# The number of tiles in a register of every engine, and the last four of 39 tiles in a branch: a GRU and mixture-of-experts kernel

## The chip, the core and the metric

The kernel runs on one core of a Trainium2 chip. The metric is the device time of one execution in microseconds; the median of several executions is compared. TensorE (PE) multiplies, VectorE (DVE), ScalarE (ACT) and GpSimd (POOL) work elementwise, and SyncE (SP) and POOL issue most of the transfers. Each engine runs its own list of instructions in order and waits on semaphores that others raise.

## What is computed

The reference runs a GRU over 8 sequences of 256 steps with 512 features, and then a mixture-of-experts layer on all 2048 hidden states:

```python
probs = softmax(x @ w_gate)                      # 8 experts
topk_w, topk_ids = top_k(probs, 2)               # two experts for each token, weights normalized
gu  = einsum('th,ehf->etf', x, w_gate_up)        # 512 -> 2*256 for each expert
eo  = einsum('eti,eih->eth', silu(g) * u, w_down)
out = x_in + routed + shared                     # shared: one dense layer of width 1024
```

The kernel computes only the two chosen experts of each token: 4096 pairs of token and expert.

## The kernel before, in words

**The GRU stage** takes most of the time: 256 steps (`step`), and between the steps the projections of later inputs, the routing of the block of 16 steps before, and the shared layer of finished blocks.

**Routing.** For each block `give_places` gives every pair a place in its expert's list, and `enter` scatters (row number, weight) into `listed` in DRAM. Each list has room for all tokens. Vacant places were filled at the start with row numbers of runs of 16 neighbouring rows and weight 0 (lines 267 to 274).

**Laying tiles.** At the end `lay_tiles` cuts the eight lists into tiles of 128 pairs. With c pairs for an expert there are ceil(c/128) tiles, and their sum depends on the data; the largest possible sum is `NT` = 39. Part 0 counts (`cnt`), turns counts into tiles (`nte`), sums them up over the experts (`cum`, whose last column is the number of all tiles), finds for each of 128 partitions, taken as tile numbers, the expert (`ex`) and the place in the list (`at`), and gathers the lists (`nT`). Part 1 spreads the expert of each tile to all partitions with a matmul of ones and writes it as integers (`steer`). Part 2 transposes the gathered lists into `row` and `share`. A tile number past the last tile of the data gets expert 7 and a vacant list.

**The stage of tiles.** All 39 tiles are run, whether or not they hold tokens. `fetch_rows(i)` gathers 128 hidden states from DRAM by `row` (POOL, `xr`). `tile_unit(i)` makes four groups of work: `before_` transposes `xr` on PE (line 766), has ACT copy it to `xrT` (768) and fetches tile i + 2; then four up products `gu_t` (659), whose weights are chosen by a register of PE loaded from `steer` (774); `turn` transposes the gated activation (670, copy 672); the two down products `yp` (785), the weighting on DVE (788) and a scatter from POOL that adds the 128 rows to `out` in DRAM (791). Each scatter waits until the one before it has landed, since both add to the same tensor.

`run_tile` sets the order by hand: in one call it issues the first group of tile i, half of the up products of tile i-1, the turn of tile i-2, the other half, and the down products of tile i-2. Two last calls with nothing new run the pipeline empty. Lists are built by Python: the program is one straight sequence, and only which expert's weights are read is decided on the chip. After the last instruction SP waits for every semaphore, each engine drains, and a barrier of all engines ends the program (line 989).

Of the kernel before, what the change touches and what calls it, by code (L numbers as in the profile page):

```python
# [9 lines left out]
F32 = mybir.dt.float32  # L10
BF16 = mybir.dt.bfloat16
I32 = mybir.dt.int32
AF = mybir.ActivationFunctionType
ALU = mybir.AluOpType
# [3 lines left out]
P = 128  # L18
# [7 lines left out]
def kernel(  # L26
# [51 lines left out]
    nc = tc.nc  # L78
    B, T, D = x.shape
    G3 = w_ih.shape[1]  # L80
    E = w_gate.shape[1]
# [7 lines left out]
    NTOK = B * T  # L89
    NT = (2 * NTOK - E) // P + E  # L90
# [12 lines left out]
    ps_mm = ctx.enter_context(tc.tile_pool(name="ps_mm", bufs=3, space=PSUM))  # L103
# [84 lines left out]
    ident = const.tile([P, P], F32, name="ident")  # L188
# [101 lines left out]
    def for_transposes(shape, name):  # L290

        spare.rotate(-1)
        n = shape[0] * (shape[1] if len(shape) > 1 else 1)
        bank = spare[0][:, 0:n]
        return bank if len(shape) == 1 else bank.rearrange("p (a b) -> p a b", b=shape[1])
# [283 lines left out]
    laid = {}  # L579

    def small(shape, tag, dtype=F32):
        return two.tile([P, *shape], dtype, tag=tag, name=tag, bufs=1)

    def lay_tiles(part_no):

        if part_no == 0:
            ps = ps_mm.tile([P, E], F32, tag="mm", name="cntp")
            nc.tensor.matmul(ps, ones, count, start=True, stop=True)
            cnt = small([E], "cnt")
            nc.vector.tensor_copy(cnt, ps)  # L590
            more = small([E, NM], "parts")
            nc.vector.tensor_tensor(
                more,
                cnt.unsqueeze(2).broadcast_to([P, E, NM]),
                full.unsqueeze(1).broadcast_to([P, E, NM]),
                ALU.is_gt,
            )
            nt = small([E], "nte")
            nc.vector.tensor_reduce(nt, more, AX.X, ALU.add)

            ee = small([E, E], "ee")
            nc.vector.tensor_tensor(ee, upto, nt.unsqueeze(1).broadcast_to([P, E, E]), ALU.mult)
            cum = small([E], "cum")
            nc.vector.tensor_reduce(cum, ee, AX.X, ALU.add)

            past = small([E], "past")
            nc.vector.tensor_scalar(past, cum, part, None, ALU.is_le)
            ex = small([1], "ex")
            nc.vector.tensor_reduce(ex, past, AX.X, ALU.add)
            spread = small([NT], "spread", BF16)  # L610
            nc.vector.tensor_scalar(spread, ident[:, 0:NT], ex, None, ALU.mult)
            nc.vector.tensor_tensor(past, past, nt, ALU.mult)
            no = small([1], "no")
            nc.vector.tensor_reduce(no, past, AX.X, ALU.add)

            nc.vector.tensor_tensor(no, part, no, ALU.subtract)
            nc.vector.scalar_tensor_tensor(no, ex, float(NM), no, ALU.mult, ALU.add)
            at = small([1], "at", I32)
            nc.vector.tensor_scalar(at, no, float(E * NM), None, ALU.min)
            got = small([P, 2], "nT")  # L620
            nc.gpsimd.indirect_dma_start(
                out=got.rearrange("i p v -> i (p v)"),
                out_offset=None,
                in_=listed.rearrange("r p v -> r (p v)"),
                in_offset=bass.IndirectOffsetOnAxis(ap=at, axis=0),
            )
            laid.update(spread=spread, got=got)
        elif part_no == 1:
            ps = ps_mm.tile([P, NT], F32, tag="mm", name="exp")
            nc.tensor.matmul(ps, ones, laid["spread"], start=True, stop=True)  # L630
            steer = small([NT], "steer", I32)
            nc.vector.tensor_scalar(steer, ps, float(E - 1), None, ALU.min)
            laid["steer"] = steer
        else:
            ps = for_transposes([2, P], "listp")
            for v in range(2):
                nc.tensor.transpose(ps[:, v, :], laid["got"][:, :, v], ident)
            row = small([NT], "row", I32)
            nc.vector.tensor_copy(row, ps[:, 0, 0:NT])
            share = small([NT], "share")  # L640
            nc.vector.tensor_copy(share, ps[:, 1, 0:NT])
            laid.update(row=row, share=share)
# [106 lines left out]
    def fetch_rows(i):  # L749
        if i < NT:  # L750
            xr_of[i] = xpool.tile([P, D], F32, tag="x", name=f"xr_{i}")
            nc.gpsimd.indirect_dma_start(
                out=xr_of[i],
                out_offset=None,
                in_=rows.rearrange("b t d -> (b t) d"),
                in_offset=bass.IndirectOffsetOnAxis(ap=laid["row"][:, i : i + 1], axis=0),
            )

    def tile_unit(i):
        box = {}  # L760

        def before_():
            ps = for_transposes([NQ, P], f"xrTp_{i}")
            xr = xr_of.pop(i)
            for q in range(NQ):
                nc.tensor.transpose(ps[:, q, :], xr[:, q * P : (q + 1) * P], ident)  # L766
            xrT = two.tile([P, NQ, P], F32, tag="xrT", name=f"xrT_{i}")
            nc.scalar.copy(xrT, ps)  # L768
            box["xrT"] = xrT
            fetch_rows(i + 2)  # L770

        def weights(w):
            if "e" not in box:
                box["e"] = nc.values_load(
                    laid["steer"][0:1, i : i + 1],
                    engines=(mybir.EngineType.PE,),
                    min_val=0,
                    max_val=E - 1,
                )
            return we[:, bass.ds(box["e"], 1), w, :].rearrange("p o n -> p (o n)")  # L780

        def done(f, lhs, rhs):
            if f == 0:
                box["y"] = ps_mm.tile([P, D], F32, tag="mm", name=f"yp_{i}")
            nc.tensor.matmul(box["y"], lhs, rhs, start=(f == 0), stop=(f == NF - 1))  # L785
            if f == NF - 1:
                y = two.tile([P, D], F32, tag="y", name=f"y_{i}")
                nc.vector.tensor_scalar(  # L788
                    y, box["y"], laid["share"][:, i : i + 1], None, ALU.mult
                )  # L790
                nc.gpsimd.indirect_dma_start(  # L791
                    out=out.rearrange("b t d -> (b t) d"),
                    out_offset=bass.IndirectOffsetOnAxis(
                        ap=laid["row"][:, i : i + 1], axis=0
                    ),
                    in_=y,
                    in_offset=None,
                    compute_op=ALU.add,
                )

        return unit(
            f"t{i}",
            box,
            lambda q: box["xrT"][:, q, :],
            lambda q: weights(q),
            lambda f: weights(NQ + f),
            done,
            before_,
        )


    queue = deque()
    under_way = {"up": None, "turn": None}
# [10 lines left out]
    def run_tile(stages):  # L824


        last, oldest = under_way["up"], under_way["turn"]
        ups = last[1] if last else []
        for work in [
            *(stages[0] if stages else []),  # L830
            *ups[: NQ // 2],
            *(oldest[2] if oldest else []),
            *ups[NQ // 2 :],
            *(oldest[3] if oldest else []),
        ]:
            work()
        under_way.update(up=stages, turn=last)
# [94 lines left out]
    for e in (E - 4, E - 3):  # L932
# [3 lines left out]
        (0, choose), (MM, sum_logits), (2 * MM, order_experts), (2 * MM, weigh), (5 * MM, give_places),  # L936
        (5 * MM, lambda k: enter(k, 0)), (5 * MM, lambda k: enter(k, 1)), (6 * MM, send_rows),
        (7 * MM, lambda k: lay_tiles(0)), (8 * MM, lambda k: load_again(k - 1)),
        (8 * MM, load_again), (14 * MM, lambda k: lay_tiles(1)),
        (22 * MM, lambda k: lay_tiles(2)),  # L940
        (22 * MM, lambda k: fetch_rows(0)), (22 * MM, lambda k: fetch_rows(1)),
    ]
# [12 lines left out]
        if loads:  # L955
            loads.popleft()()
    assert not loads
    for i in range(NT):
        run_tile(tile_unit(i))
    for _ in range(2):  # L960
        run_tile(None)
    assert not any(under_way.values())


# [28 lines left out]
```

## Time and profile before

| what | value |
|---|---|
| median of 3 runs | 1509.24 us (1508.29 to 1509.33) |
| profiled execution | 1514.91 us, its span 1513.1 us |
| PE busy | 1443.1 us, 95% of the span |
| first tile's first transpose on PE | 1271.6 us after the span's start |
| last tile's `yp` ends on PE | about 1499.7 us |
| last scatter to `out` starts on POOL | 1503.5 us |
| granted PE clock in the stage of tiles | 1.00 |

The profiled execution took 5.67 us more than the median, and 1.8 us of its time lie outside its span. Times named by line come from that one execution. The stage of tiles and what follows it fill the last 241.5 us, 16% of the span.

### The profile page before, as it was taken

To read this page: it belongs to the slowest core of one execution; us is meant where nothing else is said; L and a number is where in the kernel's file an instruction comes from. 1 tells how busy PE (TensorE), PEld (TensorE's weight loads), DVE (VectorE), ACT (ScalarE), POOL (GpSimd) and SP (SyncE) were. 2 spreads that over 40 slices of the span, in tenths; PEclk is the share of its full clock that TensorE was granted. 3 is DMA by queue.
4 is the path that set the end of the run, shared out by engine and by line. 5 is a ranking of instruction groups with operands and counts; after the bars stand their busy time and mean duration, and the time that the engine had idled before them with its cause. 6 is when DMAs were issued, how large, how long until landed. Compare 5 with 4: busy or idle time off the path is not lost.

```text
span 1513.1 us, 75290 instructions
## 1 busy us (share of the span) xinstructions
PE 1443.1 (95%) x33154; PEld 1058.3 (70%) x33154; DVE 751.6 (50%) x2782; ACT 423.4 (28%) x1786; POOL 258.6 (17%) x505
## 2 busy tenths in 40 slices
PE   4699999999999999999999999999999999999996
PEld 1487777787778787777877777877787754444442
DVE  2356555655565656465655565556565541222221
ACT  0222222333332333333333333333333311222221
POOL 1122311111100001010101010101011221444442
PEclk8799999999999999999999999999999999999998
DMA  9244522122211011111101020111011332545453
GB/s 187 83 108 120 94 57 70 49 63 71 62 51 39 19 45 35 28 49 28 50 15 38 28 56 14 35 28 42 15 48 43 97 98 77 97 85 96 85 97 49
DMA packets 70122, 92.78 MB, mean 61 GB/s; under 512 B 13538, under 2 KB 46370, under 8 KB 69796
## 3 DMA queue, kind: packets, MB, share of 16 engines
q0 software_dynamic: 16352, 39.67, 12.9%
q1 hardware_dynamic: 53056, 48.14, 12.1%
q8 instruction: 261, 4.28, 1.2%
q14 instruction: 65, 0.53, 0.1%
q10 hardware_dynamic: 388, 0.16, 0.1%
HBM read 56.55 MB, written 31.37 MB: 58 GB/s over the span
## 4 chain that ended last, share of the span: by engine, by line
PE 90%; DMA 3%; DVE 3%; issue 2%; ACT 1%; SPq 0%; ACTq 0%; POOLq 0%; DVEq 0%; POOL 0%
PE ps_r L419 16%; PE ps_n L419 15%; PE gu_s L705 15%; PE ps_z L419 14%; PE gu_t L659 9%; PE gip L310 9%; PE po L310 7%; PE yp L785 4%; DMA we<-in_L_cond_W_hh_dram 1%; DVE zT L430 1%; DMA we<-in_L_cond_W_ih_dram 1%; DVE hn L454 0%; ACT z L449 0%; DVE hT L455 0%; PE ps_z L766 0%
## 5 line engine op out<-in xcount | busy, mean ns | idle before, releaser
L419 PEld LDWEIGHTS ps_r<-we,hT 128*8 128x8 f32 x8192 | 226.1, 89 | 119.3 <-ACT ps_z L403 72.7
L419 PE MATMUL ps_r<-we,hT 128*8 128x128 f32 x8192 | 280.8, 273 | 18.4 <-DVE hT L455 11.3
L419 PE MATMUL ps_n<-we,hT 128*8 128x128 f32 x8192 | 288.6, 273 | 1.0 <-issue 0.4
L419 PE MATMUL ps_z<-we,hT 128*8 128x128 f32 x8192 | 283.7, 273 | 2.4 <-issue 2.4
L705 PE MATMUL gu_s<-hc,wsu 128*32 128x256 f32 x4096 | 250.6, 379 | 1.2 <-issue 1.1
L458 POOL COPY hc<-hT 128x32 f32<-128x32 f32 x256 | 62.7, 245 | 1054.9 <-DVE hT L455 1052.3
L419 PEld LDWEIGHTS ps_n<-we,hT 128*8 128x8 f32 x8192 | 233.6, 90 | 8.3 <-issue 7.5
L419 PEld LDWEIGHTS ps_z<-we,hT 128*8 128x8 f32 x8192 | 234.7, 90 | 3.5 <-issue 3.3
L310 PE MATMUL gip<-we,xT 128*32 128x512 f32 (+1 forms) x1976 | 197.2, 508 | 29.5 <-DVE xT L299 22.0
L438 ACT ACTIVATE r<-rT 128x32 f32<-128x32 f32 x256 | 58.5, 229 | 521.5 <-DVE rT L430 521.5
L705 PEld LDWEIGHTS gu_s<-hc,wsu 128*32 128x32 f32 x4096 | 150.9, 110 | 76.0 <-issue 14.6
L430 DVE STREAM_TRANSPOSE rT<-ps_r 128x128 f32<-128x128 f32 x256 | 80.5, 314 | 190.5 <-PE ps_r L419 190.0
L659 PE MATMUL gu_t<-we,xrT 128*128 x312 | 146.7, 593 | 0.2 <-ACT xrT L768 0.2
L430 DVE STREAM_TRANSPOSE nT<-ps_n 128x128 f32<-128x128 f32 x256 | 80.9, 316 | 121.9 <-PE ps_n L419 121.8
L310 PE MATMUL po<-wsd,act_s 128*32 128x256 f32 (+1 forms) x1408 | 137.9, 476 | 0.0
L310 PEld LDWEIGHTS gip<-we,xT 128*32 128x32 f32 x1976 | 73.7, 111 | 82.0 <-issue 63.9
L403 ACT COPY ps_n<-seed_hn 128x128 f32<-128x128 f32 x256 | 68.8, 269 | 83.4 <-DVE nT L430 80.5
L650 DVE TENSOR_TENSOR act_t<-gu_t,act_t 128x256 f32<-128x256 f32 x39 | 16.6, 425 | 146.5 <-ACT act_t L649 146.5
L430 DVE STREAM_TRANSPOSE zT<-ps_z 128x128 f32<-128x128 f32 x256 | 81.1, 317 | 11.7 <-PE ps_z L419 3.9
L791 POOL DMA_INDIRECT out_dram<-y,row x39 | 61.8, 1585 | 124.5 <-DVE y L788 114.2
L446 ACT ACTIVATE nn<-nt 128x32 f32<-128x32 f32 x256 | 58.8, 230 | 81.0 <-DVE nt L444 79.6
L659 PEld LDWEIGHTS gu_t<-we,xrT 128*128 128x128 f32 x312 | 53.3, 190 | 38.7 <-issue 38.0
(160 smaller groups left out, 1204.6 us busy)
## 6 DMA issues: line engine op xcount, KB each, us to landing
gid_rz<-gi SPq DMA_DIRECT2D x16, 512.0 KB
seeds<-gid_rz SPq DMA_DIRECT2D x256, 32.0 KB
we<-in_L_ffn_w_gate_up_dram POOLq DMA_DIRECT2D x32, 256.0 KB, 3.7
gid_n<-gi SPq DMA_DIRECT2D x16, 256.0 KB
seeds_n<-gid_n SPq DMA_DIRECT2D x256, 16.0 KB
wsu<-_L_ffn_w_sh_gate_up_dram POOLq DMA_DIRECT2D x32, 128.0 KB, 3.6
rows<-hr SPq DMA_DIRECT2D x128, 32.0 KB
we<-in_L_ffn_w_down_dram POOLq DMA_DIRECT2D x16, 256.0 KB, 4.6
```

Source lines behind the costliest of these rows:

```text
L310: nc.tensor.matmul(ps[32 * c : 32 * c + 32], lhs(c), rhs, start=start, stop=stop, skip_group_check=True,)
L403: nc.scalar.copy(banks[g][:, 0:P], src[g])
L419: nc.tensor.matmul(bank[32 * j : 32 * j + B, 0:P], hT[:, q, 0:B], whh_v[:, q, a, j, :], start=False, stop=(q == NQ - 1), skip_group_check= ...
L430: nc.vector.transpose(gT.rearrange("p a b -> p (a b)"), banks[g][:, 0:P])
L438: nc.scalar.activation(r, gr, AF.Sigmoid)
L446: nc.scalar.activation(nn, nt, AF.Tanh)
L458: nc.gpsimd.tensor_copy(hc_of_block(k).rearrange("p g q (c t) -> p q g c t", t=TS)[:, :, :, :, t], new.rearrange("p q (g c) -> p q g c", c=2),
L650: nc.vector.tensor_tensor(act, ps[:, 0:IM], act, ALU.mult)
L659: nc.tensor.matmul(box["ps"], lhs(q), w_up(q), start=(q == 0), stop=(q == NQ - 1))
L705: nc.tensor.matmul(box["ps"][32 * g : 32 * g + 32, two_i, :], wsu[c][:, q, two_i, fs], hc_of[m][:, :, q, :], start=(two_i == 0 and q == 0) ...
L785: nc.tensor.matmul(box["y"], lhs, rhs, start=(f == 0), stop=(f == NF - 1))
L791: nc.gpsimd.indirect_dma_start(out=out.rearrange("b t d -> (b t) d"), out_offset=bass.IndirectOffsetOnAxis(ap=laid["row"][:, i : i + 1], a ...
```

## The change

The tile count, `cum[:, E-1]`, gets a place beside the experts: `spread` has one more column (the count in partition 0), the matmul of ones copies it to all partitions, and it becomes column 39 of `steer`. After everything else has been issued, and ahead of the tiles, every engine loads that integer into a register (`values_load` without a list of engines). The first 35 tiles (2048*2/128 + 3) are run as before and the pipeline is run empty. Then each engine compares its register with 35: if it is greater, tiles 35 to 38 are fetched and run, and otherwise the engine jumps past them. Tiles 33 and 34 no longer fetch tiles 35 and 36; the branch does.

```diff
-            spread = small([NT], "spread", BF16)
-            nc.vector.tensor_scalar(spread, ident[:, 0:NT], ex, None, ALU.mult)
+            spread = small([NT + 1], "spread", BF16)
+            nc.vector.tensor_scalar(spread[:, 0:NT], ident[:, 0:NT], ex, None, ALU.mult)
+            nc.vector.tensor_tensor(spread[:, NT:], ident[:, 0:1], cum[:, E - 1 : E], ALU.mult)
...
-            ps = ps_mm.tile([P, NT], F32, tag="mm", name="exp")
+            ps = ps_mm.tile([P, NT + 1], F32, tag="mm", name="exp")
             nc.tensor.matmul(ps, ones, laid["spread"], start=True, stop=True)
-            steer = small([NT], "steer", I32)
-            nc.vector.tensor_scalar(steer, ps, float(E - 1), None, ALU.min)
+            steer = small([NT + 1], "steer", I32)
+            nc.vector.tensor_scalar(steer[:, 0:NT], ps[:, 0:NT], float(E - 1), None, ALU.min)
+            nc.vector.tensor_copy(steer[:, NT:], ps[:, NT:])
...
-            fetch_rows(i + 2)
+            if i + 2 not in (always, always + 1):
+                fetch_rows(i + 2)
...
-    for i in range(NT):
-        run_tile(tile_unit(i))
-    for _ in range(2):
-        run_tile(None)
-    assert not any(under_way.values())
+    tiles = nc.values_load(laid["steer"][0:1, NT : NT + 1], min_val=1, max_val=NT)
+
+    def run_tiles(first, last):
+        for i in range(first, last):
+            run_tile(tile_unit(i))
+        for _ in range(2):
+            run_tile(None)
+        assert not any(under_way.values())
+
+    always = NTOK * 2 // P + 3
+    run_tiles(0, always)
+    with tc.If(tiles > always):
+        fetch_rows(always)
+        fetch_rows(always + 1)
+        run_tiles(always, NT)
```

The way around the branch is not empty in the built program. There every engine raises its own semaphores by what the skipped instructions would have added, and POOL does it for its transfers: it first waits until all of them have landed, then adds 16 to each of its eight transfer semaphores with one instruction. The waits at the end of the program count on these sums.

## The prediction

> **What bounds the kernel now.** I read the page first for which engine is busy at the end, then the stage of tiles by groups of instructions, then the chain of waits over its last tiles, and last the records of the closing line. The groups of instructions from 1265 us on (line, engine, operation, shapes, count | busy us, mean ns | idle time before and what ended it):
>
> ```profile
> L659 PE MATMUL gu_t<-we,xrT 128*128 x312 | 146.7, 593 | 0.2 <-ACT xrT L768 0.2
> L785 PE MATMUL yp<-we,actT_t 128*128 x156 | 73.4, 593 | 0.5 <-ACT actT_t L672 0.5
> L791 POOL DMA_INDIRECT out_dram<-y,row x39 | 61.8, 1585 | 124.5 <-DVE y L788 114.2 <-DMA out_dram<-y,row 6.7 <-issue 3.7
> L752 POOL DMA_INDIRECT xr<-rows,row x36 | 35.5, 987 | 23.1 <-PE ps_z L766 12.4 <-issue 10.7
> ```
>
> The reader sees PE with 0.7 us of waits in the whole stage, while POOL waits 114 us for DVE's `y`. So in this stage PE alone sets the pace, and it is the pace of 39 tiles, because `gu_t` and `yp` are counted for 39. The chain that ended last, in order of time (start us, us, who), shows one tile's length and what follows the last tile:
>
> ```profile
> 1478.26 1.72 PE yp L785 x4
> 1479.98 0.44 PE ps_z L766 x4
> 1480.41 1.72 PE gu_t L659 x4
> 1482.13 0.22 PE ps_r L670 x2
> 1482.35 1.72 PE gu_t L659 x4
> 1484.07 1.72 PE yp L785 x4
> ...
> 1495.25 1.73 PE yp L785 x4
> 1496.98 0.02 issue
> 1497.01 0.76 DVE y L788
> 1497.77 0.34 issue
> 1498.11 4.67 DMA out_dram<-y,row
> ```
>
> From `yp` to `yp` is 1484.07 - 1478.26 = 5.81 us. The chain ends in the last two scatters, one behind the other, and then in the closing line. Records of that line (line, queue, operation, count: ns min/median/max, first and last start us):
>
> ```profile
> L989 SPq EVENT_SEMAPHORE  x12: 17/28/28, 1508.0 to 1513.1; - x12
> L989 POOLq DRAIN  x3: 46/103/9010, 1503.3 to 1512.9; - x3
> L989 SPq DRAIN  x3: 7/7/7, 1508.6 to 1512.6; - x3
> ```
>
> SP's first wait ends at 1508.0, when the last scatter has landed (it started at 1503.5). Yet the program ends at 1513.1: POOL's long drain ends at 1503.31 + 9.01 = 1512.3, some 4.3 us after the landing, and the barrier waits for it.
>
> [...] scatter records last 1.55 to 1.64 us, landing takes 4.4 to 5.0.
>
> **How many tiles hold tokens.** The time turns on this and no profile shows it, so I take it from the inputs: the reference's own GRU and router give the eight experts 498, 438, 284, 598, 362, 852, 453 and 611 pairs. That is 4+4+3+5+3+7+4+5 = 35 tiles of 128. Thirty-five is not more than 35, so the branch is jumped over. For a 36th tile the fullest last tile (498 = 3*128 + 114) would need 15 pairs more; rounding in the products doesn't move that many.
>
> **The change part by part.**
>
> *Four tiles less.* Tiles 35 to 38 take 4 x 5.81 = 23.24 us out of PE's stretch, wholly on the path. With them go four gathers (4 x 0.99) and four scatters (4 x 1.59) on POOL, their transfers, and DVE's and ACT's part; these lay beside PE and gain nothing more. The last two tiles run the pipeline empty as tiles 37 and 38 did. **-23.24.**
>
> *The last two scatters carry tokens.* Before, the last two scatters belonged to vacant tiles, whose rows lie in runs of 16; they landed in 4.67 (chain) and about 4.4 us, the least of 39, against a median of 4.9. If tiles 33 and 34 take the median, the two links grow by 0.2 and 0.5. **+0.7** (0 to 0.9).
>
> *Two small DVE operations and a 40th column.* The product for `spread` is like its 128x1 neighbours, 0.16 us, ahead of `at` (ready 1238.9). The list gather that needs `at` starts only at 1241.6, since the last `enter` must land first: 2.7 us of cover. The copy into `steer` (0.15 us) comes at 1245.6, and DVE then idles 4.4 us. **0**; uncovered 0.3.
>
> *Five register loads.* PE already loads one register for each tile: 39 loads of 0.30 to 0.84 us, 0.40 in the median, which PE's sequencer makes ahead of its queue. The new one waits for `steer` (done at 1245.6) and stands ahead of tile 0's transposes, behind the last shared products; queued behind it are those transposes. The old load for tile 0 was made at 1269.4, 2.2 us before the transposes began at 1271.6, so 0.5 us more fits in; at worst +0.6. POOL's load stands ahead of the gather of tile 2, issued at 1259.2 and needed at 1276.0: 12 us of slack after 4.9 of flight is none lost. ACT's stands ahead of `xrT` of tile 0 (idle 5.35 us before it), DVE's ahead of tile 0's gating (idle 4.7 us), SP's and its range check behind its last transfer. **0.**
>
> *Moved fetches.* Gathers 35 and 36 leave tiles 33 and 34; jumped over, they are not issued. **0.**
>
> *The branch and the way around it.* PE, ACT and DVE reach it when their last work is queued, at the latest 0.8 us after `yp`[...]. SP sits there long before. POOL reaches it as its last scatter starts: 4.4 us of cover. What is exposed comes after the landing: POOL's wait for that landing, one more wait, the addition to eight semaphores, a branch. I estimate two waits at 0.06 (SP's ten waits took 0.54 us), the addition at 0.03[...]: **+0.2**. Behind it are SP's twelve waits (0.7 us), which now begin after POOL's addition; before, SP was done 0.6 us after the landing and waited 3.7 us for POOL's drain, so that drain still covers them.
>
> *The drain.* Before, it was queued while the last scatter was not yet issued; now it stands behind the landing. I take its end to stay 4.3 us behind the end of POOL's work: **0**. If it was only riding out the scatter, it becomes as short as the other two (0.1 us); SP's waits then end last, 1.0 us after the landing: -3.4. If it takes its 9.01 us anew from its new start: +4.7.
>
> **Sum:** -23.24 + 0.7 + 0.2 = -22.3. Against the profiled execution that is 1514.9 - 22.3 = 1492.6; that execution stood 5.7 us above the median, so I take the difference off the median: 1509.24 - 22.3 = **1486.9 us**.
>
> **The rivals.**
>
> *The drain vanishes behind POOL's new wait*: 1486.9 - 3.4 = 1483.5. For it: the drain has no work of its own that the page names. Against: 4.3 us after the landing something still ran. Chance 0.12.
>
> *The way around costs*: the drain anew[...]: up to 1486.9 + 4.7 = 1491.6. Chance 0.17.
>
> *The branch is taken* (the count on the chip is 36 or more, or the column holds something else), which ends slower. PE then runs empty at 1499.7 - 23.2 = 1476.5. POOL starts scatter 34 after 3.8 us, is busy 1.6, and only then can gather tile 35, 0.3 later; it lands after 5.4 (its median): 11.1 us without work on PE. Four tiles then take 4 x 5.81 + 1.5 (39 tiles took 1271.6 to 1499.7, 228.1 = 39 x 5.81 + 1.5), so `yp` ends at 1512.3, 12.6 us later than before: 1509.24 + 12.6 = 1521.8. It decides from the 36th tile on. The counts above speak against it. Chance 0.03.
>
> **How the numbers follow.** The forecast has 0.66; some 0.02 are for what none of these names. About 0.2%, 3 us, is what a measurement of this kernel can tell from no change; every case but the taken branch is beyond that on the fast side. The range goes from the vanished drain to the costly way round: 1483.4 to 1491.8. Faster 0.96, same 0.01, slower 0.03.
>
> **What would show it.** `gu_t` and `yp` counted for 35 tiles (x280 and x140), still 5.81 us from `yp` to `yp`, and the last `yp` ending near 1476.5 in the span. Five register loads besides 35 on PE, none with a wait of PE, ACT or DVE behind it. The last two scatters landing in about 4.9 us. After the last landing 5.3 us to the end of the span, POOL's long drain in it: 9 us or 1 us there decides between the first two rivals. Wrong at the root: x312 again, and a hole of 11 us in PE ahead of tile 35.

## The result, and the profile after

The changed kernel took **1489.09 us** in the median of four runs (1485.87 to 1490.79), the kernel before 1509.28 us beside it. The ratio is 0.9861 with a 95% interval of 0.9843 to 0.9879, that is 20.2 us less (18 to 24). The forecast was 1486.9 us, with a range of 1483.4 to 1491.8: faster, as forecast, by some 2 us less than forecast.

The two profiled executions (1485.87 and 1514.91 us) differ by 29 us, more than the medians do. Most of the surplus lies ahead of the tiles: the first transpose of tile 0 starts at 1263.1 us in the changed kernel and at 1271.6 us in the kernel before. A second profile of the kernel before has it at 1275.7, and two kernels below whose code is the old one up to that point have it at 1264.8 and 1275.1. I take the difference for chance between executions, since 7.7 of its 8.5 us are there already at the last GRU step, up to which the two programs have the same text, and since the kernel before took 1504.27 to 1510.12 us in eleven executions on one chip. It is not shown that the change has no part in it: where both kinds were profiled in one set, the changed front was the earlier one (1262.7 in e2 against 1264.8 in e1; 1271.5 in e7 against 1275.1 and 1275.7 in e6 and e8). The medians of three sets, 20.2, 21.7 and 20.3 us less than before, against the 20.9 that the stages add up to below, leave little room for a part of several microseconds. So I compare from that transpose on.

The groups of instructions of the changed kernel from 1257 us on, with the columns of the groups shown before:

```profile
L661 PE MATMUL gu_t<-we,xrT 128*128 x280 | 131.7, 593 | 0.2 <-ACT xrT L770 0.2
L788 PE MATMUL yp<-we,actT_t 128*128 x140 | 65.9, 593 | 0.5 <-ACTq L974 0.5
L794 POOL DMA_INDIRECT out_dram<-y,row x35 | 55.5, 1585 | 113.2 <-DVE y L791 95.9 <-DMA out_dram<-y,row 13.7 <-issue 3.7
L754 POOL DMA_INDIRECT xr<-rows,row x32 | 31.5, 985 | 21.0 <-PE ps_z L768 11.6 <-issue 9.4
```

The counts are those of 35 tiles (8 and 4 for each), one matmul takes 593 ns as before, and PE still waits only 0.7 us. The 0.5 us at `yp` are as long as before and named otherwise: the trace now puts them down to ACT's way around, whose semaphore record (1465.9) follows directly on ACT's last copy.

The chain of waits of the changed kernel over its last tiles (start us, us, who):

```profile
1452.34 1.72 PE yp L788 x4
...
1458.15 1.72 PE yp L788 x4
...
1463.52 1.73 PE yp L788 x4
1465.25 0.02 issue
1465.27 0.76 DVE y L791
1466.04 0.59 issue
1466.62 4.79 DMA out_dram<-y,row
```

A tile takes 1458.15 - 1452.34 = 5.81 us, unchanged, and the chain leaves PE for the last two scatters as it did before. New is what POOL does at the branch's line. Records of that line on POOL's queue (operation, count: ns min/median/max, first and last start us):

```profile
L974 POOLq EVENT_SEMAPHORE  x4: 17/43/43, 1472.1 to 1477.1; - x4
L974 POOLq COMPARE_BRANCH  x1: 53/53/53, 1471.9 to 1471.9; - x1
L974 POOLq INC_SWDGE_SEM  x1: 1319/1319/1319, 1477.2 to 1477.2; - x1
```

I read `INC_SWDGE_SEM` as the addition to the eight transfer semaphores. It starts 0.2 us after the last landing (1477.02) and takes 1.32 us. Then the closing line of the changed kernel:

```profile
L1004 SPq EVENT_SEMAPHORE  x14: 17/28/28, 1478.5 to 1484.0; - x14
L1004 POOLq DRAIN  x3: 46/103/4684, 1478.6 to 1483.8; - x3
```

SP's waits begin only when the addition is done (1478.5; before, at the landing), and POOL's long drain takes 4.68 us from there to 1483.25. From the last landing to the end there are 0.20 + 1.32 + 0.03 + 4.68 + 0.83 (the rest of the barrier) = 7.06 us, where the kernel before had 5.15.

The same four stretches, worked out from the records of each profiled execution (us; the landing is the last update of the scatter's semaphore):

| kernel | first transpose to last `yp` | `yp` to last scatter | its landing | landing to end |
|---|---|---|---|---|
| before | 228.09 | 3.85 | 4.44 | 5.15 |
| before, again (e8) | 228.09 | 3.84 | 4.79 | 5.15 |
| changed | 204.85 | 4.21 | 4.86 | 7.06 |
| changed, again (e2) | 204.85 | 3.75 | 4.79 | 7.06 |
| changed, third (e10) | 204.85 | 4.28 | 4.85 | 7.06 |
| 35 tiles written out (e1) | 204.85 | 3.85 | 4.88 | 4.83 |
| 35 tiles and an empty branch (e3) | 204.85 | 3.82 | 4.79 | 4.85 |
| branch in front (e4) | 206.29 | 3.85 | 4.82 | 4.85 |
| branch in front, gathers ahead (e5) | 204.87 | 3.91 | 4.84 | 4.85 |
| the same, again (e9) | 204.87 | 3.98 | 4.88 | 4.85 |
| 35 tiles, fills on POOL last (e6) | 204.85 | 4.11 | 4.79 | 13.66 |
| changed, fills ahead of the branch (e11) | 204.85 | 4.37 | 4.85 | 14.98 |
| branch taken (e7) | 243.71 | 3.95 | 4.63 | 5.18 |

The stretch of the tiles and the last column repeat to within 0.03 us between profiles of one kernel; the two in the middle scatter by half a microsecond.

### The profile page after: what moved, and what is told of

It reads as the page before. It is cut to its first block, busy times and chain, and to the rows that moved or that the text cites. A ratio compares the mean times of both kernels' runs of the same rounds, so it can differ in the third digit from the quotient of the medians.

```text
span 1484.1 us, 75080 instructions
## 1 busy us (share of the span) xinstructions
PE 1411.5 (95%) x33082; PEld 1029.6 (69%) x33082; DVE 744.3 (50%) x2772; ACT 418.2 (28%) x1774; POOL 248.0 (17%) x497
## 3 DMA queue, kind: packets, MB, share of 16 engines
q1 hardware_dynamic: 53056, 48.14, 12.6%
q8 instruction: 261, 4.28, 1.2%
## 4 chain that ended last, share of the span: by engine, by line
PE 90%; DMA 3%; DVE 3%; issue 2%; ACT 1%; SPq 0%; POOL 0%; DVEq 0%; ACTq 0%; POOLq 0%
PE ps_r L419 16%; PE gu_s L707 15%; PE ps_n L419 15%; PE ps_z L419 15%; PE gip L310 9%; PE gu_t L661 8%; PE po L310 7%; PE yp L788 4%; DMA we<-in_L_cond_W_hh_dram 1%; DMA we<-in_L_cond_W_ih_dram 1%; DVE zT L430 1%; DVE hn L454 0%; ACT z L449 0%; DVE hT L455 0%; PE ps_z L768 0%
## 5 line engine op out<-in xcount | busy, mean ns | idle before, releaser
L419 PEld LDWEIGHTS ps_r<-we,hT 128*8 128x8 f32 x8192 | 222.4, 89 | 120.8 <-ACT ps_z L403 72.0
L419 PE MATMUL ps_z<-we,hT 128*8 128x128 f32 x8192 | 279.3, 273 | 3.2 <-issue 3.2
L419 PE MATMUL ps_n<-we,hT 128*8 128x128 f32 x8192 | 277.9, 273 | 0.0
L419 PEld LDWEIGHTS ps_z<-we,hT 128*8 128x8 f32 x8192 | 229.8, 90 | 4.7 <-issue 4.3
L419 PEld LDWEIGHTS ps_n<-we,hT 128*8 128x8 f32 x8192 | 229.8, 90 | 0.2
L707 PEld LDWEIGHTS gu_s<-hc,wsu 128*32 128x32 f32 x4096 | 140.3, 110 | 84.8 <-issue 16.1
L310 PE MATMUL po<-wsd,act_s 128*32 128x256 f32 (+1 forms) x1408 | 134.2, 476 | 0.0
L661 PE MATMUL gu_t<-we,xrT 128*128 x280 | 131.7, 593 | 0.2 <-ACT xrT L770 0.2
L794 POOL DMA_INDIRECT out_dram<-y,row x35 | 55.5, 1585 | 113.2 <-DVE y L791 95.9
L403 ACT COPY ps_r<-seeds 128x128 f32<-128x128 f32 x256 | 67.0, 262 | 18.8 <-DMA seeds<-gid_rz 18.6
```

The lines of the kernel that those rows point to most:

```text
L310: nc.tensor.matmul(ps[32 * c : 32 * c + 32], lhs(c), rhs, start=start, stop=stop, skip_group_check=True,)
L403: nc.scalar.copy(banks[g][:, 0:P], src[g])
L419: nc.tensor.matmul(bank[32 * j : 32 * j + B, 0:P], hT[:, q, 0:B], whh_v[:, q, a, j, :], start=False, stop=(q == NQ - 1), skip_group_check= ...
L661: nc.tensor.matmul(box["ps"], lhs(q), w_up(q), start=(q == 0), stop=(q == NQ - 1))
L707: nc.tensor.matmul(box["ps"][32 * g : 32 * g + 32, two_i, :], wsu[c][:, q, two_i, fs], hc_of[m][:, :, q, :], start=(two_i == 0 and q == 0) ...
L794: nc.gpsimd.indirect_dma_start(out=out.rearrange("b t d -> (b t) d"), out_offset=bass.IndirectOffsetOnAxis(ap=laid["row"][:, i : i + 1], a ...
```

## Experiments: what the way around the branch costs

My theory after the result: the four tiles gave their 23.24 us, and the addition with the drain behind it took some 2 us back. The rivals: the loads and branches themselves cost something on the way, or the drain alone has grown.

**e1: 35 tiles written out, without loads and branch.** The kernel before with

```diff
-            fetch_rows(i + 2)
+            if i + 2 < 35:
+                fetch_rows(i + 2)
-    for i in range(NT):
+    for i in range(35):
```

It serves only data with at most 35 tiles, such as these.

> The kernel before with 35 tiles written into the program: no count, no register, no branch; tiles 35 to 38, which hold no tokens, are left out. It is the gain alone. If what the changed kernel gives back lies in the way around the branch (from the landing of the last scatter to the end of the span: 7.1 us in the changed kernel, 5.2 before), this one has 5.2 us there, and the PE stretch and the two last scatters of the changed kernel: about 1.9 us less than the changed kernel, 21.4 less than before. If the give-back came from elsewhere (the loads, the longer lists), the stretch after the landing is 7 us here too, or PE's stretch of tiles is shorter than the changed kernel's.

**e2: the changed kernel again**, on the same chip.

> The changed kernel once more, on the same chip as its comparisons. Expected: 20.5 us less than before by the stages (23.2 of PE less 0.8 of scatters less 1.9 after the landing), about 1488.8; if its profiled execution's 29 us less were the rule, 1480.

Measured: e1 1485.18 us, ratio to before 0.9855 (0.9838 to 0.9873); e2 1485.53 us, 0.9864 (0.9844 to 0.9883); before 1507.26. The medians, 0.35 us apart, can't tell the two apart, since the two intervals are over 5 us wide each. The profiles can: the stretch of the tiles is 204.85 us in both, and the landing is followed by 4.83 us in e1 (5.2 were expected) and 7.06 in e2. Ahead of the tiles, from the last GRU step's activation to tile 0's first transpose, they take 49.21 and 49.28 us. The closing line of e1:

```profile
L990 SPq EVENT_SEMAPHORE  x12: 17/28/28, 1478.4 to 1483.2; - x12
L990 POOLq DRAIN  x3: 46/103/9125, 1473.3 to 1482.9; - x3
```

Here the drain again stands ahead of the landing: queued at 1473.29, it ends at 1482.41, 4.02 us after the landing. So what the changed kernel has besides 35 tiles costs 7.06 - 4.83 = 2.2 us after the last landing, and no more than 0.1 us from the last GRU step to the tiles. Of the 2.2 us some 1.55 are the wait and the addition, and 0.66 come from the drain, which takes 4.68 us behind them instead of ending 4.02 us behind the landing.

**e3: the branch with next to nothing in it.** Loads, compares and jumps stay; the tiles in the branch are gone, and with them the transfers that the way around must make up for:

```diff
     with tc.If(tiles > always):
-        fetch_rows(always)
-        fetch_rows(always + 1)
-        run_tiles(always, NT)
+        nc.vector.memset(laid["share"], 0.0)
```

> The changed kernel with another branch body: one small memset on DVE in place of the four tiles (jumped over all the same, since 35 tiles hold tokens). The five loads, the five compares and the jump stay; POOL has no transfers to make up for. If the addition to the transfer semaphores and the drain behind it are what costs, the stretch from the last landing to the end is 5.2 us again, 1.9 less than in the changed kernel. If the compare and the jump[...] cost it, it stays near 7.

Measured in one run: 1480.98 us, with the first transpose as early as 1260.9, so the total says little. After the landing there are 4.85 us, as in e1, and the profile has no addition behind the tiles. Five loads, five compares and the jumps cost nothing that shows; the 2.2 us belong to what must be made up for when tiles are skipped.

**e6: work on POOL behind the last scatter.** Is the drain tied to the last scatter, or does it cost by itself? e1 with

```diff
+                if i == 34:
+                    for _ in range(14):
+                        nc.gpsimd.memset(y, 0.0)
```

after the scatter. The fills must wait until the scatter has read `y`, so they begin at the landing (in e11 below, which has the same fills, the first starts at 1477.77, 0.05 us after it).

> 35 tiles written in, and after the last scatter 14 memsets of its source tile on POOL, which must wait for the scatter's landing: POOL works some 5 to 8 us longer past the landing. It asks what POOL's long drain waits for. If it rides out something that the last scatter started (in four profiles it ended 8.8 to 8.9 us after that scatter began), the drain is short here, under 0.3 us, because that time has passed. If a drain costs over 4 us by itself once POOL has issued scatters, as the 4.7 us behind the addition in the changed kernel suggest, it ends over 4 us after the last memset.

Its closing line:

```profile
L993 POOLq DRAIN  x3: 46/103/5249, 1496.5 to 1502.3; - x3
```

The kernel took 1504.43 us in one run. The last fill ends at 1497.04, over 8 us after the landing (1488.90), and the drain at 1501.75. So the last drain ends 4.7 us behind POOL's last work, fills here and the addition in the changed kernel, also where the last transfer landed long before; it is not the rest of a transfer. It is no fixed price of every drain: POOL's drain at the start of the program takes 0.18 us, before and in the changed kernel. What the 4.7 us consist of stays open.

**e11: the same fills between the last scatter and the branch of the changed kernel.** The additions in e4 and e5 below took 0.73 and 0.79 us, so 1.32 could have contained a rest of the landing.

> The changed kernel with 14 fills of y (0.52 us each) on POOL between the last scatter and the branch, so that the addition comes some 8 us after the last landing. If the addition's 1.32 us is its own work, it stays at 1.3 us. If the half of it is a rest of the last transfer (the additions in front of the tiles took 0.73 and 0.79 us), it falls to 0.7 or 0.8 us. In both, the drain behind it takes 4.7 us, as it did behind the addition and behind the fills of the kernel of 35 tiles; should the drain follow the landing instead, it is under 1 us here.

One run took 1494.50 us. The addition, on POOL's queue at the branch's line:

```profile
L977 POOLq INC_SWDGE_SEM  x1: 1319/1319/1319, 1485.8 to 1485.8; - x1
```

and the drain on its closing line:

```profile
L1007 POOLq DRAIN  x3: 46/103/4684, 1487.2 to 1492.4; - x3
```

8.1 us after the landing both have the length they have in the changed kernel, 1319 and 4684 ns. So the addition's 1.32 us contain no rest of the landing. Why it is shorter ahead of the tiles is open.

## Experiments: the branch in another place, and the branch taken

**e4: the branch ahead of tile 0**, with the gathers of tiles 0 and 1 behind it, so that addition and landing would be over long before the end:

```diff
-        (22 * MM, lambda k: fetch_rows(0)), (22 * MM, lambda k: fetch_rows(1)),
...
-    run_tiles(0, always)
     with tc.If(tiles > always):
...
         run_tiles(always, NT)
+    fetch_rows(0)
+    fetch_rows(1)
+    run_tiles(0, always)
```

> The branch with tiles 35 to 38 stands ahead of tile 0 in place of behind tile 34; gathers 0 and 1 follow it. If the way around costs only because nothing runs beside it, it now lies under the last shared products on POOL (gather 0 had 10 us of slack), the stretch after the last landing is 5.2 us, and the kernel is 1 to 2 us faster than the changed one; PE pays for waiting until its own queue is empty, up to 1 us ahead of tile 0. If POOL's way round is longer than the slack, PE stands idle ahead of tile 0 by more than 2 us and nothing is won.

Measured: 1491.59 us (six runs), ratio 0.9904 (0.9885 to 0.9922), 6.1 us above e2 on the same chip. Who waited longest from 1255 to 1275 us in e4 (us in total, times, longest):

```profile
POOL xr L754 <- PEq L972: 26.1, 1, 26.1
...
PE ps_n L768 <- DMA xr<-rows,row: 6.7, 1, 6.7
```

The end is short again (4.85 us), but the gather of tile 0 waits for a semaphore that PE raises on its own way around the branch. PE's queue comes there only when the shared products are done, at 1262.9, so the gather is issued at 1263.3, and PE stands 6.7 us without work. And the hole costs more than its length. The same profile in stretches (us, then busy time and count of PE, PEld, DVE, ACT, POOL, then the granted clock):

```profile
1260.00:1262.80 2.80, 2.80 (x28) 0.65 (x20) 0.69 (x1) 0.00 (x0) 0.00 (x0) 1.00 0.03 6
1269.50:1271.80 2.30, 2.14 (x8) 1.46 (x9) 0.00 (x0) 0.59 (x1) 0.86 (x1) 0.50 0.38 151
1271.80:1275.00 3.20, 3.19 (x6) 1.52 (x7) 0.00 (x0) 0.59 (x1) 1.03 (x2) 0.82 0.58 154
```

After the hole PE works at half its clock (granted 0.50, for 3.4 us), which makes the stretch of the tiles 206.29 - 204.85 = 1.4 us longer. By stages against e2: 6.8 later start of tile 0 (49.3 us after the last step's activation in e2, 56.05 here), 1.4 of clock, 2.1 less at the end: +6.1, as timed. The expected gain of 1 to 2 us did not come.

**e5 and e9: the branch ahead of tile 0, with the gathers of tiles 0 to 2 issued before it.** As e4, but these gathers stand among the shared products, and the skipped tiles fetch their rows into another pool:

```diff
         (22 * MM, lambda k: fetch_rows(0)), (22 * MM, lambda k: fetch_rows(1)),
+        (22 * MM, lambda k: fetch_rows(2)),
...
+            if i >= always:
+                fetch_rows(i)
...
-            if i + 2 not in (always, always + 1):
+            if 2 < i + 2 < always:
...
-    run_tiles(0, always)
     with tc.If(tiles > always):
-        fetch_rows(always)
-        fetch_rows(always + 1)
         run_tiles(always, NT)
+    run_tiles(0, always)
```

> The branch ahead of tile 0 again, but gathers 0, 1 and 2 stay ahead of the branch, so that no tile waits for a gather that waits for the branch; tiles 35 to 38 gather into another buffer. If the front branch lost its 6.4 us on PE only because gather 0 was held back behind the branch of the other engines, PE's hole ahead of tile 0 is now under 1 us, the stretch after the last landing 4.85 us, and the kernel 1.2 to 2 us faster than the changed one and 1 us slower than 35 tiles written in. If waiting for PE's empty queue is the cost, the hole stays over 2 us and the place behind the last tile is the better one.

e5 took 1494.38 us where the kernel before took 1517.10: ratio 0.9849 (0.9824 to 0.9874). To set it against the changed kernel itself, both ran again on one chip:

> The branch ahead of tile 0 and the three first gathers issued before it, as in the earlier run of this form, now beside the changed kernel on one chip. Theory (the way around costs 2.2 us behind the last landing, and nothing in front when the gathers are under way): landing to end 4.85 us against 7.06, stretch of the tiles 204.9 us in both, and a median 1.5 to 2.2 us under that of the changed kernel. Rival (the front loses as much as the end saves): the first transpose stands over 1.5 us later behind the last GRU step than in the changed kernel, and the medians agree within 0.7 us.

> The changed kernel, beside the one above. Both theories: landing to end 7.06 us with the addition at 1.32 us and the drain at 4.68 us, and 20 to 21 us under the kernel before.

Measured: e9 1490.41 us, 0.9865 (0.9843 to 0.9887); e10 1491.08 us, 0.9871 (0.9848 to 0.9894). The closing line of e9 has the long drain ahead of the landing again:

```profile
L1006 POOLq DRAIN  x3: 46/109/9125, 1475.1 to 1484.7; - x3
```

By the profiles e9 gains 2.2 us behind the landing and 0.3 in the start of the last scatter, and its first transpose stands 49.88 us behind the last step where e10 has 49.28, a loss of 0.6, of which PE waits 0.5 for its own way around: 1.9 us in all. The theory's 1.5 to 2.2 us is met by stages, but the medians differ by 0.7 us only, with intervals that overlap almost wholly. So e9 is the better order by its trace and not shown to be faster.

**e7: the branch taken.** The same data, and the branch entered from the 35th tile on, so that all 39 are run as two pieces:

```diff
-    with tc.If(tiles > always):
+    with tc.If(tiles > always - 1):
```

> The changed kernel with the comparison at 34 in place of 35, so that the branch is taken: tiles 35 to 38 run, vacant as before, behind an empty pipeline. The prediction's third rival says 12.6 us more than before, about 1520, with 11 us without work on PE ahead of tile 35. [...] If the gather of tile 35 overlaps what runs out, less.

**e8: the kernel before**, beside it.

> The kernel before, profiled once more. If the 7.7 us by which the changed kernel's last GRU step came earlier in the two profiles (1213.8 against 1221.5 us) are chance and no effect of the change, this one's last GRU step lies near the 1212 to 1216 of the other profiles, its stage of tiles takes PE 228.1 us again, and its last landing is 5.2 us ahead of the end.

Measured: e7 1531.76 us (four runs), ratio 1.0095 (1.0072 to 1.0118) to the kernel before, 14.7 us slower; e8 1519.32 in one run. In e8 the stretch of the tiles (228.09 us) and the time behind the landing (5.15) are as expected, but its last GRU step came at 1225.4 us and not near 1212 to 1216. What PE waited for in e7 from 1470 to 1516 us:

```profile
PE ps_r L768 <- DMA xr<-rows,row: 11.8, 1, 11.8
```

and e7 in stretches, across the hole and after it:

```profile
1471.00:1476.30 5.30, 4.78 (x13) 1.80 (x11) 1.60 (x3) 0.76 (x2) 0.24 (x1) 1.00 0.41 53
1476.40:1488.10 11.70, 0.00 (x0) 0.00 (x0) 0.74 (x1) 0.00 (x0) 5.70 (x5) 0.66 0.51 92
1490.10:1492.90 2.80, 2.80 (x4) 1.25 (x5) 0.00 (x0) 0.58 (x1) 0.35 (x1) 0.50 0.32 94
1492.90:1495.50 2.60, 2.60 (x7) 1.08 (x7) 0.00 (x0) 0.00 (x0) 0.00 (x0) 0.84 0.00 0
1495.50:1501.30 5.80, 5.80 (x20) 2.83 (x19) 1.70 (x4) 1.73 (x4) 0.00 (x0) 1.00 0.00 0
```

PE is empty for 11.8 us, because POOL gets to the gather of tile 35 only behind its scatter. The forecast for this case had 11.1, near it in part by luck: the scatter started 5.3 us after the last `yp` instead of 3.8, and the gather landed after 4.6 us instead of 5.4. The four tiles then take 27.1 us instead of the 24.7 of the forecast (4 x 5.81 + 1.5), since the clock stays at 0.50 until about 1493.7. The granted clock was 0.50 after both holes, of 6.7 us in e4 and 11.8 in e7; counted from PE's first work after the hole, it stayed there for 3.4 us in e4 and 5.6 in e7. Why the two differ is not shown. The terms add up: 204.85 + 11.77 + 27.09 = 243.71 us is e7's stretch of the tiles, 15.6 more than before.

## Why the prediction was right, step by step

**Four tiles less, -23.24: right.** 228.09 - 204.85 = 23.24 us. The pace, the count and the flow out of the pipeline are as the chain before showed them.

**The count of tiles, 35: right.** `gu_t` is counted 280 times, and POOL went the way around.

**The last two scatters, +0.7: too large, the sign likely but not shown by the changed kernel alone.** The price came from one scatter of the kernel before that landed in 4.44 us; in e8 the same one took 4.79. From the last `yp` to the landing the two profiles of the kernel before take 8.29 and 8.63 us, the three of the changed kernel 9.07, 8.54 and 9.13. That is +0.45 in the mean, but the two groups overlap. Over all profiles above, ten with 35 tiles have 8.85 us in the mean (8.54 to 9.22) and three with 39 have 8.50 (8.29 to 8.63). That vacant rows are the cause was not tried.

**Loads and columns, 0: right.** Records of the load's line (queue, operation, count: ns, start us):

```profile
L963 POOLq TENSOR_LOAD <-steer x1: 499/499/499, 1248.7 to 1248.7; - x1
L963 ACTq TENSOR_LOAD <-steer x1: 464/464/464, 1258.1 to 1258.1; - x1
L963 PEldq TENSOR_LOAD <-steer x1: 482/482/482, 1260.4 to 1260.4; - x1
L963 DVEq TENSOR_LOAD <-steer x1: 542/542/542, 1263.3 to 1263.3; - x1
L963 SPq TENSOR_LOAD <-steer x1: 2110/2110/2110, 1264.7 to 1264.7; - x1
```

PE's is over at 1260.9 while PE multiplies shared products until 1263.2, and tile 0's transposes follow without a gap. SP's 2.1 us lie where SP has nothing left to issue (its last transfer starts at 1264.0). e1, without loads and column, is only 0.07 us quicker from the last GRU step to tile 0 (49.21 against 49.28).

**The branch itself, covered: right.** The trace of before records no branch, so what one costs was not shown when the forecast was made. In the changed kernel compare and jump took 45 to 72 ns on four engines and 378 ns on PE. PE's lies at 1466.1, while PE still multiplies the last `yp` (to 1467.95); e3, with all five, has 4.85 us behind the landing where e1 without them has 4.83, so none of the five shows there.

**The way around, +0.2: the step that failed.** The estimate had 0.03 us for the addition to eight semaphores; it took 1.32 us, the same in each of four profiles. The trace of before has one such instruction, at the very start of the program, and it takes just the time of the estimate. The traces of e4 and e5 have one ahead of the tiles. In this order (operation, count: ns, start us):

```profile
L980 POOLq INC_SWDGE_SEM  x1: 31/31/31, 0.1 to 0.1; - x1
L972 POOLq INC_SWDGE_SEM  x1: 728/728/728, 1244.2 to 1244.2; - x1
L977 POOLq INC_SWDGE_SEM  x1: 788/788/788, 1263.6 to 1263.6; - x1
```

The instruction's length isn't fixed, and 0.03 us holds where POOL has issued nothing yet. Before these three and the 1.32 us of the changed kernel POOL had issued 0, 137, 140 and 207 transfers. The length rises with their number, though not in proportion; whether they are the reason was not tried. The term should have had a range of its own.

**The drain, 0: right in kind, 0.3 us short.** "Its end stays 4.3 us behind the end of POOL's work" was the choice among three. Measured are 4.71 us behind the addition. The forecast's short drain (-3.4) and the 9.01 us anew (+4.7) are both excluded by the 4.68 of the changed kernel, and e6 agrees: the last drain ends 4.7 us behind POOL's last work. The 9 us of the record before were about half waiting for the landing, and then such a stretch: in all eight profiles with the drain queued ahead of the landing it ends 4.0 to 4.35 us behind the landing, whenever that comes.

**SP's waits, covered: right.** They end at 1479.3, 4 us ahead of the drain.

The sum as it should have been: -23.24 + 0.45 + 1.9 = -20.9 us, against -22.3 forecast and -20.2 measured (18 to 24). Against 35 tiles written out the way around costs 2.2 us, not 1.9, since there the drain ends 4.0 us behind the landing, against 4.35 with 39 tiles (before, e8, and also e7 with 39). Where these 0.3 us come from was not tried.

**The rivals.** "The way around costs" had the right place, behind the last landing, but not the cause: the drain was not taken anew at 9.01 us (it took 4.68), and POOL's compare and jump took 53 ns. The addition was the larger part. "The drain vanishes" is excluded. "The branch is taken" forecast 12.6 us more than before; e7 gave 14.7 timed and 15.6 in its profile. Its missing terms are the half clock after the hole, 2.4 us, and 0.7 us more of hole.

## What to carry to other kernels

The jump past the data-dependent branch cost little here (compare and jump took 45 to 378 ns on the five engines, and behind the last landing nothing of it shows, 4.85 us in e3 against 4.83 in e1); what the way around must make up for cost more (2.2 us), above all transfers issued by POOL, for which it waits and adds to their semaphores (1.32 us), and at the end of this kernel that is fully exposed. The price of an instruction that a trace shows in one place only, such as the empty start of a program, gets a range when it is carried to another place. And a branch is a seam: gathers issued behind it instead of before it left PE empty for 6.7 us (e4) and 11.8 us (e7), and PE then ran at a granted clock of 0.50 for 3.4 and 5.6 us more.

## What the runs showed that I had not expected

The addition to eight transfer semaphores takes 1.32 us behind the tiles (four profiles) and 0.73 to 0.79 us ahead of them (three), and the same kind of instruction at the start of the program takes 0.03; the reason is open. POOL's last drain ends 4.7 us behind POOL's own work where that came last, and 4.0 (35 tiles) to 4.35 us (39) behind the landing where that came last. A register load takes 0.46 to 0.54 us on four engines and 2.1 us on SP. PE's compare took 378 ns where it jumped; in e7, where it entered the branch, PE's two records of that line took 84 and 185 ns.
